# Attention over two layers: image 0 starts from centred values, and the last checks move ahead of the last residual

## The chip, the cores and the metric

The kernel runs on one core of a Trainium2 chip. A core has TensorE for matrix products, VectorE, ScalarE and GpSimd for work on elements, and a sync engine, SP, that here only issues transfers. The engines run side by side, each through its own list of instructions in order, and wait for one another by semaphores. Products land in PSUM; everything else lies in SBUF. The metric is the time of one execution on the device, in microseconds. Smaller is better.

## The reference

The input `x` holds 16 images of 256 channels by 32 x 32 places. Two layers of the same form follow, each with its own weights:

```python
x = x + attention(group_norm(x), Wq, bq, Wk, bk, Wv, bv, rel_h, rel_w)

def group_norm(v, G=16, eps=1e-5):       # groups lie along the last axis
    g = v.reshape(B, H, W, G, C // G)
    m = mean(g, axis=(1, 2, 4)); s = var(g, axis=(1, 2, 4))
    return (g - m) / sqrt(s + eps)

def attention(x):                         # 4 heads of depth 64, n = 1024 places
    q, k, v = Wq @ x + bq, Wk @ x + bk, Wv @ x + bv
    sim = einsum('bhdi,bhdj->bhij', q, k)
    qpos = einsum('hdi,bhdj->bhij', rel_h + rel_w, q)
    return v @ softmax(sim + qpos).T
```

All is float32. The axis that the norm groups is the image's last one, of 32, so a group takes two columns of the picture in all channels.

## The kernel before

A unit is one image in one layer: 32 units, in an order (`units`, line 141) that begins with images 0 to 3 in layer 0. A unit has two pairs of heads, a pair two halves of 512 queries; so a unit has four blocks, and `block(n)` (line 619) writes down the work of one. All instructions are recorded in the order in which the code calls them (`tc.manual_schedule`), and each engine runs its own in that order. Nothing is rearranged.

In a block, `seed` (line 344) has VectorE write the positional part of 128 rows of scores into PSUM, `scores` (line 373) has TensorE add q times k on top and ScalarE take the exponential, and `add_up` (line 397) sums the exponentials on VectorE. `attend` (line 409) multiplies the exponentials by the values. The next block's or unit's projections are put between these by `prepare` (line 593): `project` (q and k, line 258), `values` (line 286), `positions` (line 314). Each is cut in two stretches. A second stretch waits for a `token`, a small GpSimd memset that waits for the first stretch (`stretches`, line 157). PSUM is used as four buffers of two banks with the tags a, b, c and d, handed round in the order of the list `ring`.

The group norm of a unit is prepared one or two units ahead, in pieces on ScalarE: sums of a group (`norm_sums`), squares around the mean (`norm_squares`), and the scaling itself (`norm_apply`). The sums over partitions are small products with a constant matrix (`norm_mean`, `norm_var`), and the power of −0.5 is taken on GpSimd (line 237).

Units 0 and 1 cannot be prepared so. Lines 840 to 959 are the start. SP issues the loads in the order image 0, Wq and Wk of layer 0, image 1, both layers' Wv, Wq and Wk of layer 1, then the small ones and image 2. VectorE sums image 0's halves (`reduced`), two products give the mean (`first_mean`), ScalarE negates it and takes squares of 10 groups, VectorE centres all values and takes the squares of 6. The variance, the power (line 901) and the scaling of the centred values follow (lines 924 to 930), and only then `q(0)` (line 938), the first projection. The weights come untransposed; `transposed` turns them on TensorE and `taken` has ScalarE copy them to SBUF. Image 1's mean and variance are done in the same way in this start, half of its squares on VectorE, and its values are applied by ScalarE in blocks 0 and 1; image 2's sums are ScalarE's in the same blocks.

The last two blocks have a version of their own, `block_without_pieces` (line 762). In the last one, TensorE sums the last exponentials into `pd`. VectorE takes the reciprocal of them (line 827), ScalarE copies them to `d`, and SP sends two rows of `d` to `den_all`, where all softmax denominators are kept. VectorE then ends the last half of the residual (`finish_half`, line 556), which is stored, and checks that the denominators lie in range (`in_range`, line 565). A product over partitions counts the good ones, and a cast writes `flag` (line 837). All engines load the flag; if a denominator was out of range, `general_path` does everything again in a slower way.

Of the kernel before, what the change touches and what calls it, by code (L numbers as in the profile page):

```python
# [9 lines left out]
F32 = mybir.dt.float32  # L10
# [7 lines left out]
P = 128  # L18
# [34 lines left out]
def fast_path(ctx, tc, sh, x, layers, out, W, den_all, token, good, flag):  # L53
# [67 lines left out]
    def transposed(tag, raw, parts):  # L121
        ps = psum2(tag, raw.name + "_t")
        for a in range(2):
            for cc in range(CC):
                for oc in range(CC):
                    nc.tensor.transpose(
                        ps[:, a, cc * C + oc * P : cc * C + (oc + 1) * P],
                        raw[:, a, oc * C + cc * P : oc * C + (cc + 1) * P],
                        W.ident,
                    )  # L130
        for a, which in enumerate(parts):
            raw_t[which] = ps[:, a, :]

# [60 lines left out]
    def norm_sums(u, gs):  # L194
        if u not in reds:
            reds[u] = small.tile([P, G], F32, tag="red", name=f"red_{u}")
        for g in gs:
            of_group(u, g, AF.Identity, reds[u])
# [27 lines left out]
    def norm_squares(u, gs):  # L226
        for g in gs:
            of_group(u, g, AF.Square, sums[u], bias=negs[u][:, g : g + 1])
# [16 lines left out]
    def norm_apply(u, gs):  # L245
        rstd, shift = rss[u]
        for g in gs:
            nc.scalar.activation(  # L248
                grouped(xns[u], g),
                grouped(xt[units[u][0]], g),  # L250
                AF.Identity,
                bias=shift[:, g : g + 1],
                scale=rstd[:, g : g + 1],
            )
# [142 lines left out]
    def add_up(blk, j):  # L397
        u, pr, half = blk
        if j == 0:
            return  # L400
        if j == 1:
            accs[blk] = apool.tile([P, 2, HALF], F32, tag="acc", name=f"acc_{u}_{pr}_{half}")
            nc.vector.tensor_tensor(accs[blk], probs[blk, 0], probs[blk, 1], ALU.add)  # L403
        else:
            nc.vector.tensor_tensor(accs[blk], accs[blk], probs[blk, j], ALU.add)  # L405
# [150 lines left out]
    def finish_half(u, pr, half, o, rden):  # L556
        b, l = units[u]
        columns = slice(half * HALF, (half + 1) * HALF)
        xs = xt[b][:, pr, columns]
        y = outs[u, pr][:, half, :]  # L560
        nc.vector.tensor_tensor(y, o, rden, ALU.mult)
        nc.vector.scalar_tensor_tensor(xs, y, W.bv[l][:, pr : pr + 1], xs, ALU.add, ALU.add)
        nc.sync.dma_start(flat(out[b, pr * P : (pr + 1) * P])[:, columns], xs)
# [24 lines left out]
    ring = ["b", "c", "a", "d"]  # L588
# [29 lines left out]

    def block(n):
# [27 lines left out]
        for j in range(1, 4):  # L647
            scores(blk, j)
        (first, first_out), (second, second_out) = prepare(u, b)
        first(0)  # L650
        if b == 0 and one:
            norm_apply(u + 1, range(0, 1))
        if b == 1 and two:
            norm_sums(u + 2, range(9, 11))
# [3 lines left out]
        if b == 0 and one:  # L658
            norm_apply(u + 1, range(1, 5))
        if b == 1 and two:  # L660
            norm_sums(u + 2, range(11, 12))
        if b == 2 and two:
            norm_squares(u + 2, range(0, 5))
# [21 lines left out]
        add_up(blk, 2)  # L685
        if half == 0:
            second(1)
            second_out()
# [13 lines left out]
        if b == 0 and one:  # L702
            norm_apply(u + 1, range(5, 9))
        if b == 0 and two:
            norm_sums(u + 2, range(0, 2))
        if b == 1 and two:
            norm_sums(u + 2, range(12, G))
        if b == 1 and one:
            norm_apply(u + 1, range(9, 11))
        if b == 2 and two:  # L710
            norm_squares(u + 2, range(5, 11))
# [8 lines left out]
        if after:  # L720
            scores(after, 0)
        values_of_p.word()
# [10 lines left out]
        if two and half == 1:  # L733
            mean_out()
# [10 lines left out]
        if b == 0 and two:  # L745
            norm_sums(u + 2, range(2, 9))
        if b == 1 and one:
            norm_apply(u + 1, range(11, G))
        if b == 2 and two:
            norm_squares(u + 2, range(11, G))  # L750
# [11 lines left out]
    def block_without_pieces(n, half):  # L762
# [61 lines left out]
        finish_half(u, pr, 0, outs[u, pr][:, 0, :], rdens[u, pr][:, :HALF])  # L824
# [3 lines left out]
        d = ppool.tile([P, 2, HALF], F32, tag="p", name=f"d_{n + 1}")[:, 0, :]  # L828
# [3 lines left out]
        finish_half(u, pr, 1, po[:, :, :QUART], rden)  # L832
# [3 lines left out]
        nc.tensor.matmul(pc, good[:, 3:4], W.ones[:, 0:1], start=True, stop=True)  # L836
        nc.vector.tensor_copy(flag, pc)


    load_x(0)  # L840
    raw0 = load_raw("raw0", [(0, "Wq"), (0, "Wk")])
    load_x(1)
    raw1 = load_raw("raw1", [(0, "Wv"), (1, "Wv")])
# [8 lines left out]
    def spread(t, g0=0, g1=G):  # L852
        return (
            t[:, g0:g1].unsqueeze(1).unsqueeze(3).to_broadcast([P, CC * sh.W, g1 - g0, GT])
        )

    def reduced(u, cc):
        nc.vector.tensor_reduce(
            reds[u][:, cc, :],
            xt[units[u][0]][:, cc, :].rearrange("p (w g t) -> p g w t", g=G, t=GT),  # L860
            AX.XY,
            ALU.add,
        )

    def first_mean(u, pm):
        red = reds.pop(u)
        for cc in range(CC):
            nc.tensor.matmul(pm, W.avg, red[:, cc, :], start=(cc == 0), stop=(cc == CC - 1))
        negs[u] = small.tile([P, G], F32, tag="neg", name=f"neg_{u}")
        nc.scalar.mul(negs[u], pm, -1.0)  # L870
        sums[u] = small.tile([P, G], F32, tag="sum", name=f"sum_{u}")
        xns[u] = gnpool.tile([P, CC, N], F32, tag="gn", name=f"xn_{u}")

    def centred(u, g0, g1):
        nc.vector.tensor_tensor(
            by_group(xns[u], g0, g1),
            by_group(xt[units[u][0]], g0, g1),
            spread(negs[u], g0, g1),
            ALU.add,
        )  # L880

    def rest_of_squares(u, g0):

        sq = ppool.tile([P, 2, HALF], F32, tag="p", name=f"first_sq_{u}")
        sq = sq.rearrange("p a n -> p (a n)")[:, : CC * sh.W * (G - g0) * GT].rearrange(
            "p (w g t) -> p w g t", g=G - g0, t=GT
        )
        nc.vector.tensor_tensor(sq, by_group(xns[u], g0), by_group(xns[u], g0), ALU.mult)
        nc.vector.tensor_reduce(
            sums[u][:, g0:], sq.rearrange("p w g t -> p g w t"), AX.XY, ALU.add  # L890
        )

    def first_var(u, pm):
        nc.tensor.matmul(pm, W.avg, sums.pop(u), start=True, stop=True)
        var = small.tile([P, G], F32, tag="var", name=f"var_{u}")
        nc.vector.tensor_scalar(var, pm, EPS, None, ALU.add)
        return var

    def first_rstd(u, var):
        rstd = small.tile([P, G], F32, tag="rstd", name=f"rstd_{u}")  # L900
        nc.gpsimd.tensor_tensor(rstd, var, W.mhalf[:, :G], ALU.pow)  # L901
        return rstd

    for u in range(2):
        reds[u] = small.tile([P, CC, G], F32, tag="first_red", name=f"first_red_{u}")
    G1, G2 = G // 2 + 2, G // 4
    pm0 = psum2("c", "pm_0")
    for cc in range(CC):
        reduced(0, cc)
    first_mean(0, pm0[:, 0, :G])  # L910
    transposed("a", *raw0)
    norm_squares(0, range(G1))
    centred(0, 0, G)
    rest_of_squares(0, G1)
    rstd0 = first_rstd(0, first_var(0, pm0[:, 1, :G]))
    taken(raw0[1])
    transposed("b", *raw1)
    taken(raw1[1])
    pm1 = psum2("d", "pm_1")
    for cc in range(CC):  # L920
        reduced(1, cc)
    first_mean(1, pm1[:, 0, :G])
    transposed("a", *raw2)
    for g in range(G2):
        nc.scalar.activation(
            grouped(xns[0], g), grouped(xns[0], g), AF.Identity, scale=rstd0[:, g : g + 1]
        )
    nc.vector.tensor_tensor(  # L928
        by_group(xns[0], G2), by_group(xns[0], G2), spread(rstd0, G2), ALU.mult
    )  # L930
    taken(raw2[1])
    norm_squares(1, range(0, G // 2))
    centred(1, G // 2, G)
    rest_of_squares(1, G // 2)
    (q, q_out), (k, k_out) = (
        project(0, 0, which, psum2(tag, f"p{which}_0_0")) for which, tag in (("q", "b"), ("k", "c"))
    )
    q(0)
    k(0)
    q(1)  # L940
    q_out()
    k(1)
    k_out()
    ab, ab_out = positions(0, 0, psum2("a", "pa_0_0"))
    ab(0)
    ab_out()
    var1 = first_var(1, pm1[:, 1, :G])
    for j in range(3):
        seed(blocks[0], j, ring[j])
    v, v_out = values(0, 0, psum2("d", "pv_0_0"))  # L950
    v(0)
    scores(blocks[0], 0)
# [3 lines left out]
    rstd1 = first_rstd(1, var1)  # L956
    shift1 = small.tile([P, G], F32, tag="nshift", name="nshift_1")
    nc.vector.tensor_tensor(shift1, negs.pop(1), rstd1, ALU.mult)
    rss[1] = (rstd1, shift1)
# [282 lines left out]
```

## Time and profile before

| What | us |
|---|---|
| Median of 3 runs (2536.82 to 2538.13) | 2537.84 |
| The profiled execution | 2537.8 |
| Its span, first instruction to last | 2535.9 |
| TensorE products busy in the span | 2512.9 (99%) |
| VectorE busy | 2267.8 (89%) |
| ScalarE busy | 1949.0 (77%) |
| GpSimd busy | 834.1 (33%) |
| First product of q | at 18.09 |
| Last product of values | ends at 2526.06 |
| Flag written | at 2530.28 |

Times in a trace are microseconds from the start of the span. A row of the timeline has the start, the length, the engine, the line, the operation with what it writes and reads, how many were merged, and in brackets how long the engine had been idle before and what ended that. PE is TensorE, PEld its weight loads, DVE is VectorE, ACT is ScalarE, POOL is GpSimd, and SPq the issue of a transfer. An fp32 product leaves two records. The chain of waits goes back from the last instruction, at each step to what released it.

The landing of the first transfers, from the trace (issue, and from issue to landing): image 0's halves 0.75 + 3.7 and 1.2 + 4.5, Wq 1.67 + 4.9, Wk 2.15 + 5.5, image 1's first half 2.66 + 6.3, the first Wv 3.66 + 7.3.

### The profile page before, as it was taken

Reading aid. Unit: us, or ns where it says so; the run is one execution under the profiler, and the core shown is the slowest. Engines: PE = TensorE matmul, PEld = TensorE weight load, DVE = VectorE, ACT = ScalarE, POOL = GpSimd, SP = SyncE. Lnnn points to the kernel's source line nnn. Section 1 sums busy time; section 2 is a strip of 40 time slices with the busy share of each in tenths; the row PEclk is TensorE's granted clock in tenths of the full one; section 3 lists DMA queues with packets and bytes.
Section 4 is the critical chain, followed back from the end, with each engine's and each line's share of the span. In section 5 each row is a group of like instructions: output and inputs, shape, how many; then the busy total and the mean of one; then the engine's idle time right before and its main releaser. Section 6 shows DMA issues by size and latency. Waiting matters only on the chain.

```text
span 2535.9 us, 85952 instructions
## 1 busy us (share of the span) xinstructions
PE 2512.9 (99%) x37462; PEld 1332.5 (53%) x37462; DVE 2267.8 (89%) x2133; ACT 1949.0 (77%) x3876; POOL 834.1 (33%) x1195
## 2 busy tenths in 40 slices
PE   8999999999999999999999999999999999999998
PEld 4555555555555555555555555555555555555554
DVE  6898998989989989899899899998998999989997
ACT  6778777787777887777877778877778777787654
POOL 1333333323333233333233332333323333323320
PEclk9999999999999999999999999999999999999999
DMA  3344443544444445444444444444454444444442
GB/s 90 74 79 75 87 87 67 101 96 93 96 90 104 80 76 101 88 84 95 92 88 94 79 97 81 85 104 90 87 112 81 90 79 84 80 84 77 95 81 69
DMA packets 119841, 221.57 MB, mean 87 GB/s; under 512 B 53913, under 2 KB 55449, under 8 KB 119457
## 3 DMA queue, kind: packets, MB, share of 16 engines
q0 software_dynamic: 53712, 130.10, 31.4%
q1 hardware_dynamic: 65744, 85.90, 12.0%
q8 instruction: 295, 4.83, 0.8%
q14 instruction: 90, 0.73, 0.1%
HBM read 51.78 MB, written 17.30 MB: 27 GB/s over the span
## 4 chain that ended last, share of the span: by engine, by line
PE 97%; DVE 1%; DMA 1%; POOL 1%; issue 1%; SPq 0%; ACT 0%; POOLq 0%; DVEq 0%; ACTq 0%
PE ps L385 34%; PE po L419 34%; PE pk L268 9%; PE pv L298 9%; PE pq L268 9%; PE pa L326 2%; DMA stack<-stack 0%; DMA den_all<-d 0%; PE pm L209 0%; DMA x<-in_x_dram 0%; DVE acc L405 0%; DVE rden L827 0%; POOL rstd L237 0%; POOL rstd L901 0%; POOL stack L460 0%
## 5 line engine op out<-in xcount | busy, mean ns | idle before, releaser
L349 DVE TENSOR_TENSOR ps<-abt 128x1024 f32<-128x1024 f32 x1018 | 1228.8, 1230 | 230.3 <-ACT p L394 144.3
L394 ACT ACTIVATE p<-ps,shift 128x1024 f32<-128x1024 f32 x1024 | 1091.3, 1114 | 335.4 <-PE ps L385 335.4
L385 PE MATMUL ps<-q,k 64*64 64x512 f32 x8192 | 985.9, 590 | 0.0
L419 PE MATMUL po<-p,v 64*64 64x256 f32 x16384 | 930.5, 376 | 0.0
L419 PEld LDWEIGHTS po<-p,v 64*64 64x64 f32 x16384 | 629.1, 133 | 364.3 <-issue 77.2
L405 DVE TENSOR_TENSOR acc<-acc,p 128x1024 f32<-128x1024 f32 x643 | 780.4, 1214 | 8.2 <-ACT p L394 1.4
L385 PEld LDWEIGHTS ps<-q,k 64*64 64x64 f32 x8192 | 306.6, 133 | 397.9 <-issue 274.9
L166 POOL MEMSET token<- 1x1 f32 x320 | 36.2, 113 | 1033.5 <-PE po L419 469.9
L465 POOL DMA_DIRECT2D stack<-stack x310 | 255.0, 823 | 196.0 <-DMA stack<-stack 109.4
L298 PE MATMUL pv<-Wv,xn 64*64 64x256 f32 x4096 | 244.3, 376 | 0.6 <-POOL token L166 0.3
L268 PE MATMUL pq<-xn,Wq 64*64 64x512 f32 x2048 | 243.8, 591 | 0.3 <-DVE xn L928 0.3
L268 PE MATMUL pk<-xn,Wk 64*64 64x512 f32 x2048 | 242.8, 589 | 0.0
L460 POOL DMA_DIRECT2D stack<-acc x248 | 221.6, 1075 | 41.6 <-issue 30.0
L248 ACT ACTIVATE xn<-x,nshift,rstd 128x128 f32<-128x128 f32 x496 | 210.3, 496 | 1.1 <-POOL nshift L239 1.1
L298 PEld LDWEIGHTS pv<-Wv,xn 64*64 64x64 f32 x4096 | 153.5, 133 | 102.7 <-issue 51.6
L436 POOL DMA_DIRECT2D acc<-p x124 | 118.8, 958 | 247.3 <-ACT od L480 162.3
L190 ACT ACTIVATE junk<-x,neg 128x128 f32<-128x128 f32 x498 | 195.2, 400 | 0.0
L480 ACT COPY od<-po 128x512 f32<-128x512 f32 x127 | 74.3, 585 | 114.9 <-PE po L419 114.9
L403 DVE TENSOR_TENSOR acc<-p,p 128x1024 f32<-128x1024 f32 x128 | 155.8, 1217 | 0.0
L441 POOL DMA_DIRECT2D acc<-acc x124 | 106.0, 855 | 148.3 <-DMA acc<-p 139.3
L268 PEld LDWEIGHTS pq<-xn,Wq 64*64 64x64 f32 x2048 | 78.6, 134 | 142.1 <-issue 133.2
L190 ACT ACTIVATE junk<-x 128x128 f32<-128x128 f32 x480 | 145.0, 311 | 0.0
(75 smaller groups left out, 1124.5 us busy)
## 6 DMA issues: line engine op xcount, KB each, us to landing
acc<-p POOLq DMA_DIRECT2D x124, 512.0 KB, 5.7
rden<-rd SPq DMA_DIRECT2D x126, 256.0 KB, 6.0
acc<-acc POOLq DMA_DIRECT2D x124, 256.0 KB, 3.6
x<-in_x_dram SPq DMA_DIRECT2D x32, 512.0 KB, 4.3
stack<-acc SPq DMA_DIRECT2D x248, 64.0 KB, 2.1
stack<-acc POOLq DMA_DIRECT2D x248, 64.0 KB, 3.0
out_dram<-x SPq DMA_DIRECT2D x31, 512.0 KB, 3.8
stack<-stack POOLq DMA_DIRECT2D x62, 128.0 KB, 4.2
```

The costliest lines, as they stand in the source:

```text
L190: nc.scalar.activation(junk, grouped(xt[units[u][0]], g), func, accum_out=into[:, g : g + 1], **bias)
L248: nc.scalar.activation(grouped(xns[u], g), grouped(xt[units[u][0]], g), AF.Identity, bias=shift[:, g : g + 1], scale=rstd[:, g : g + 1],)
L268: yield nc.tensor.matmul(pk[c, nh, :], w[l][rs, cc, c0 : c0 + D], xns[u][rs, cc, nh * HALF : (nh + 1) * HALF], start=(t == 0 and cc == 0), ...
L298: yield nc.tensor.matmul(pv[c, a, i, :], xns[u][rs, cc, j0 : j0 + D], W.wv[l][rs, cc, :], start=(t == 0 and cc == 0 and i == 0), stop=(t = ...
L349: nc.vector.tensor_tensor(ps.rearrange("p h (w y) -> p h w y", y=H), ab[:, :, :H].unsqueeze(2).to_broadcast([P, 2, XH, H]), ab[:, :, H + h ...
L385: nc.tensor.matmul(ps[c, h, :], a[hs, j0 : j0 + D], b[hs, columns], start=bool(tag) and i == 0, stop=i == len(terms) - 1, skip_group_check ...
L394: nc.scalar.activation(p, ps, AF.Exp, bias=W.shift)
L403: nc.vector.tensor_tensor(accs[blk], probs[blk, 0], probs[blk, 1], ALU.add)
L405: nc.vector.tensor_tensor(accs[blk], accs[blk], probs[blk, j], ALU.add)
L419: yield nc.tensor.matmul(po[c, a, :QUART], vts[u][rs, j, c0 : c0 + D], p[rs, h, a * QUART : (a + 1) * QUART], start=(t == 0 and j == 0), s ...
L460: nc.gpsimd.dma_start(at, acc[R:D, h, :], accum_op=ALU.add)
L465: nc.gpsimd.dma_start(stack[:rows_], stack[rows_ : 2 * rows_], accum_op=ALU.add)
```

## The change

At the start:

- SP loads both Wv before image 1.
- `transposed` becomes a generator, `transposes`. Wq's transposes stand between the two products of the first mean, Wk's behind the second.
- `q(0)` and the other three projection stretches of unit 0 read the centred, not the scaled values. The scaling by 1/sqrt(var) is a VectorE product from PSUM to SBUF per 512 columns (`scaled`), and the bias is added in place by ScalarE (`biased`). This is possible because a column of q or k depends on one column of the values alone, and a column lies in one group.
- The centred values themselves are scaled by VectorE in two halves (`first_scaled`), before `values` reads them.
- ScalarE takes squares of 9 groups, not 10, and copies Wq and Wk in between them.
- Image 1's mean is taken by `norm_mean`; all its squares are ScalarE's, 3 groups in the start and 13 in block 0. Its variance is taken in block 0 and its values are applied in block 1 alone.
- Image 2's sums are VectorE's: a reduction in block 0, one in block 1.
- The transposes of layer 1's Wq and Wk come behind the positions of unit 0.
- Tags: `ring` starts as c, a, b, d.

In the blocks, the calls for the norms are gathered in `norms(u, b, i)` with tables. From unit 1 on they are the old ones, but that in a unit's first block two sums come ahead of four applies.

At the end, the check of the denominators and the product that counts them come before the last half's residual. The cast of the flag comes between that residual's two VectorE instructions. `d` takes a buffer of another pool.

```diff
 def norm_apply(u, gs):
-        rstd, shift = rss[u]
         for g in gs:
+            rstd, shift = rss[u]
...
+    APPLY = {0: (0, 1, 5, 9, 9), 1: (9, 9, 9, 11, G)}
+    SUMS = {0: (0, 0, 0, 2, 9), 1: (9, 11, 12, G, G)}
+    SQUARES = {2: (0, 0, 5, 11, G)}
+    FIRST_SQUARES = {0: (3, 5, 9, G, G)}
+    FIRST_APPLY = {1: (0, 1, 4, 8, G)}
+
+    def norms(u, b, i):
+        def groups(table):
+            return range(*table.get(b, (0,) * 5)[i : i + 2])
+        if u == 0:
+            norm_squares(1, groups(FIRST_SQUARES))
+        elif u + 2 < NU:
+            norm_sums(u + 2, groups(SUMS))
+        if u + 1 < NU:
+            norm_apply(u + 1, groups(APPLY if u > 0 else FIRST_APPLY))
+        if u + 2 < NU:
+            norm_squares(u + 2, groups(SQUARES))
...
-        for j in range(1, 4):
+        for j in range(1 if n > 0 else 2, 4):
             scores(blk, j)
         (first, first_out), (second, second_out) = prepare(u, b)
         first(0)
+        norms(u, b, 0)
+        if n == 1:
+            reduced(2, 1)
+            added(2)
         seed(blk, 4, f1)
         scores(blk, 4)
         add_up(blk, 1)
+        norms(u, b, 1)
...
         add_up(blk, 2)
+        if n == 0:
+            reduced(2, 0)
...
         if after:
             scores(after, 0)
+        if n == 0:
+            mean_out = norm_var(1, filled(f1, f"pm_{n}", EPS / 2))
         values_of_p.word()
...
         rden = rdens[u, pr][:, HALF:]
         nc.vector.reciprocal(rden, pd)
-        d = ppool.tile([P, 2, HALF], F32, tag="p", name=f"d_{n + 1}")[:, 0, :]
+        d = apool.tile([P, 2, HALF], F32, tag="acc", name=f"d_{n + 1}")[:, 0, :]
         nc.scalar.copy(d, pd)
         for hs in QUARTERS:
             nc.sync.dma_start(den_all[hs, n, :], d[hs.start : hs.start + 1, :])
-        finish_half(u, pr, 1, po[:, :, :QUART], rden)
         list(in_range(flatden[:, 8 * (n - 1) :], 2))
         nc.vector.tensor_reduce(good[:, 3:4], good[:, 0:3], AX.X, ALU.min)
         pc = psum2(f1, "pc")[0:1, 0, 0:1]
         nc.tensor.matmul(pc, good[:, 3:4], W.ones[:, 0:1], start=True, stop=True)
+        steps = finish_half(u, pr, 1, po[:, :, :QUART], rden)
+        next(steps)
         nc.vector.tensor_copy(flag, pc)
+        list(steps)
...
     load_x(0)
     raw0 = load_raw("raw0", [(0, "Wq"), (0, "Wk")])
+    raw1 = load_raw("raw1", [(0, "Wv"), (1, "Wv")])
     load_x(1)
-    raw1 = load_raw("raw1", [(0, "Wv"), (1, "Wv")])
...
+    def scaled(into, t, rstd):
+        shape = dict(g=G, t=GT)
+        nc.vector.tensor_tensor(
+            into.rearrange("p (w g t) -> p w g t", **shape),
+            t.rearrange("p (w g t) -> p w g t", **shape),
+            spread(rstd, XH),
+            ALU.mult,
         )
...
+    def first_mean(pm, between):
+        part = parts.pop(0)
         for cc in range(CC):
+            nc.tensor.matmul(pm, W.avg, part[:, cc, :], start=(cc == 0), stop=(cc == CC - 1))
+            next(between)
...
+    pm0 = psum2("d", "pm_0")
     for cc in range(CC):
         reduced(0, cc)
+    first_mean(pm0[:, 0, :G], transposes("a", *raw0))
+    transposed("b", *raw1)
+    norm_squares(0, range(4))
     taken(raw0[1])
+    norm_squares(0, range(4, G // 2 + 1))
+    nc.vector.tensor_tensor(
+        by_group(xns[0]), by_group(xt[0]), spread(negs[0], CC * sh.W), ALU.add
+    )
+    rest_of_squares(G // 2 + 1)
+    pq, pk = psum2("c", "pq_0_0"), psum2("a", "pk_0_0")
+    q, k = project(0, 0, "q", pq)[0], project(0, 0, "k", pk)[0]
+    q(0)
+    q.word()
+    nc.tensor.matmul(pm0[:, 1, :G], W.avg, sums.pop(0), start=True, stop=True)
+    var = small.tile([P, G], F32, tag="var", name="var_0")
+    nc.vector.tensor_scalar(var, pm0[:, 1, :G], EPS, None, ALU.add)
+    rstd = small.tile([P, G], F32, tag="rstd", name="rstd_0")
+    nc.gpsimd.tensor_tensor(rstd, var, W.mhalf[:, :G], ALU.pow)
+    taken(raw1[1])
     for cc in range(CC):
         reduced(1, cc)
+    added(1)
+    pm1 = filled("d", "pm_1", 0.0)
     k(0)
     q(1)
     k(1)
+    kqs = {}
+    for which, bias, ps in (("q", W.bq, pq), ("k", W.bk, pk)):
+        t = kqs[which] = kqpool.tile([P, N], F32, tag=which, name=f"{which}_0_0")
+        for nh in range(NH):
+            scaled(t[:, nh * HALF : (nh + 1) * HALF], ps[:, nh, :], rstd)
...
+    biased("q", W.bq, 0)
+    biased("q", W.bq, 1)
+    biased("k", W.bk, 0)
+    qs[0, 0], ks[0, 0] = kqs["q"], kqs["k"]
+    mean_out = norm_mean(1, pm1)
+    ab, ab_out = positions(0, 0, psum2("b", "pa_0_0"))
     ab(0)
     ab_out()
+    biased("k", W.bk, 1)
+    mean_out()
...
+    first_scaled(0)
+    transposed("d", *raw2)
+    taken(raw2[1])
+    seed(blocks[0], 0, ring[0])
+    scores(blocks[0], 0)
+    seed(blocks[0], 1, ring[1])
+    seed(blocks[0], 2, ring[2])
     v, v_out = values(0, 0, psum2("d", "pv_0_0"))
     v(0)
+    norm_squares(1, range(3))
+    first_scaled(1)
+    scores(blocks[0], 1)
     v(1)
     v_out()
     seed(blocks[0], 3, ring[0])
```

## The prediction

> **What bounds the kernel now.** I read the chain of waits first, then the busy time by stretches, and only then the start and the end in order of time. The page's chain:
>
> ```profile
> PE 97%; DVE 1%; DMA 1%; POOL 1%; issue 1%; SPq 0%; ACT 0%; POOLq 0%; DVEq 0%; ACTq 0%
> ```
>
> Busy time by stretches (stretch, its length, then each engine's busy us and count, clock, DMA):
>
> ```profile
> 0.00:20.00 20.00, 9.91 (x46) 7.79 (x50) 13.20 (x15) 11.01 (x40) 3.62 (x7) 1.00 0.71 235
> ...
> 180.00:2400.00 2220.00, 2219.62 (x33308) 1173.80 (x33304) 2006.23 (x1885) 1742.80 (x3505) 763.68 (x1084) 1.00 0.45 88
> ...
> 2520.00:2536.00 16.00, 6.25 (x86) 3.07 (x77) 8.08 (x11) 0.58 (x1) 0.09 (x1) 0.78 0.20 71
> ```
>
> TensorE works 2219.62 of 2220 us in the middle. No edit there can give or take anything unless it stops TensorE. So a change is worth what it does before TensorE first runs without a break and after its last product. The chain at the start (start, us, what):
>
> ```profile
> 1.21 4.55 DMA x<-in_x_dram
> ...
> 7.92 2.30 DVE xn L875
> ...
> 11.24 0.96 DVE sum L889
> ...
> 13.22 2.94 POOL rstd L901
> ...
> 16.19 1.77 DVE xn L928
> ...
> 18.09 2.99 PE pq L268 x16
> 21.09 1.72 PE pk L268 x16
> ...
> 35.03 1.73 PE pv L298 x32
> ```
>
> From 18.09 us TensorE hardly waits again; until then it waits for image 0's normalisation, whose longest links are the power on GpSimd and the scaling after it. I use 35.03 us, where block 0's second value product begins, as a milestone: the work behind it is the same in both kernels. The end, in order of time:
>
> ```profile
> 2525.94 0.58 ACT L829 COPY d<-pd 128x512 f32<-128x512 f32 x1 [7.50 <-DVE rden L827]
> 2526.55 1.12 SPq L831 DMA_DIRECT2D den_all<-d  x2
> ...
> 2527.76 0.54 SPq L563 DMA_DIRECT2D out_dram<-x  x1
> 2528.98 0.17 DVE L568 TENSOR_SCALAR range<-den_all 128x16 f32<-128x16 f32 x1 [1.38 <-DMA den_all<-d]
> ...
> 2530.13 0.15 DVE L837 CAST flag<-pc 1x1 int32<-1x1 f32 x1 [0.37 <-PE pc L836]
> ```
>
> The last residual and its store run while VectorE would wait for `den_all` anyway. Between the flag (2530.28) and the end of the span (2535.94) lie 5.66 us, in which all engines load the flag and branch; TensorE's branch alone took 3.92.
>
> **What the Trainium skill says.** (1) "TensorE: Matmul & The Clock Gate", Part 1: TensorE runs at half rate until a free-running window of about 3.4 us has been busy. The trace agrees: the first stretch of q, 16 records, took 2.81 us (18.09 to the next group's 20.90), the following ones 1.72. (2) "VectorE: DVE Perf Modes", Why PSUM operands drop a tier: fp32 runs at one element a cycle from PSUM. The trace agrees: 128x512 products took 0.684 us from SBUF and 0.691 from PSUM, so scaling q and k in PSUM costs no more than elsewhere. (3) "GPSIMD Engine Reference", table of specifications: GpSimd shares SBUF interfaces with VectorE, and VectorE instructions with two SBUF inputs contend. The trace fits: the power took 2.93 us beside reductions, 3.54 beside seeds, and 4.06 in the median later. In the new start it again stands beside reductions, so I take 2.94.
>
> **The change part by part, the start.** Up to the first half's mean product (5.76) nothing changes.
> *Wq's transposes between the halves.* They are put in front of the second mean product in TensorE's order. Wq was issued at 1.67 and landed 4.9 us later, at 6.57. Eight transposes took 1.95 us, so 0.22 each; with a weight load of 0.21 ahead, four end at 7.72. The second mean product goes from 7.06 to 7.72: −mean starts at 8.36, not 7.70. Loss 0.66. Bounds: 0 if Wq lands at 6.0, 1.2 if at 7.1.
> *Wv ahead of image 1 on SP.* The bytes are the same; Wv lands where image 1's first half did (8.96 before), image 1 by about 11.8. Wv's transposes then follow Wk's without a wait: 0.44 for the mean product, 12 x 0.22, ends at 10.8. Image 1 is wanted only at 14. Cost nothing; if Wv came 1 us late, q would start 0.5 late.
> *q starts on centred values.* Centring takes 2.29: 8.58 to 10.87. Four squares at 0.39 and Wq's copy end at 10.7. q's first stretch starts at 10.95 instead of 18.09: 7.1 us earlier. How long it takes depends on the clock: 1.72 full, about 3.4 half. TensorE is dense from 6.84, so a full busy window ends between 10.0 and 13.5; I take 12.3, thus 2.4 us, to 13.35.
> *The variance.* ScalarE now has nine squares and both copies, ending 13.15, VectorE's seven groups 13.1; both are covered by q. The variance product queues behind q: 13.35, 0.6 with its result, var 0.17, power 14.2 to 17.15. k's and q's stretches cover it: 13.8 + 2 x 1.72 = 17.25. k's second stretch waits for a token that stands behind the power on GpSimd: 17.4 to 19.1.
> *Scale and bias after the product.* Added are four VectorE products (0.6 apart, from L561's row) and four ScalarE biases of 0.57, for two of 1.11. q's halves are ready at 19.35 and hold the positions (from 19.4, after 0.26 for image 1's mean) by nothing; they end at 20.3. k's halves, the abt copy (1.0) and k's last bias lie behind one another on ScalarE: 20.6, 21.6, 22.1. VectorE scales half of xn (2 x 0.6) before the first seed: 22.0 to 23.2. So TensorE, which had no gap here before, has one from 20.3 to 23.25, of which Wq1's and Wk1's moved transposes fill at most 1.8.
> *From there.* Scores 0.86, values 1.72, scores 0.86; the second value stretch waits for xn's other half behind two seeds (23.2 + 2 x 1.14 + 1.25 = 26.7), 1.73; two scores 1.72: 30.15 at the milestone, 4.9 us ahead of 35.03.
> *Image 1's squares and applies, image 2's sums in blocks 0 and 1.* Seven squares (2.73) behind the last exponential hold the new variance product by 0.2, and it takes 0.26. VectorE gets two reductions of 1.21 each. Block 0's stands ahead of seed 6, and VectorE idled 1.81 us before seed 7: covered. Block 1's stands ahead of seed 4, where 1.95 idled; but VectorE enters block 1 later too, since seeds 1 to 3 now stand behind the reduction of the variance, which waits for its product. Together seeds 6 and 7 come about 0.95 later against TensorE, and they had 0.7 and 0.4 of slack: 0.6 lost. About 1.1 in all; between 0.3 and 1.6. The two reordered ScalarE pieces in later units (sums ahead of four applies) have cover from 4.3 us of products and cost nothing.
> Sum of the start: −4.9 + 1.1 = −3.8.
>
> **The end.** The copy `d` still waits for the reciprocal: both read `pd`, and in both built orders its wait is on VectorE alone; its new pool's older transfers are long done. So `den_all` lands as before and the checks still start at 2528.98. Now the product (0.69) stands ahead of the flag's cast, less the 0.37 that the cast waited for `pc`: flag 0.4 later. The store, issued at 2527.76 before, follows at about 2531.6 behind SP's flag load; with 2.2 us to landing it ends at 2533.8, and SP's closing waits by about 2535, when TensorE's branch ends too. Cost 0.5; bounds 0.3 and 1.5.
> Total −3.8 + 0.5 = −3.3. The profiled execution took 2537.8 with its span of 2535.9, so 1.9 lie around it, and it equals the median of 2537.84: 2534.5 us. That is 0.13%; 0.2%, or 5.1 us, is about what a measurement of this kernel can tell from no change, so I call it within.
>
> **Rivals.**
> *More at the start.* If Wq lands early (−0.6), block 1's seeds fit into VectorE's 1.95 us of idle there (−0.6) and the clock is free at 10 (−0.2), then −4.7 to −5.8: about 2532.4. For it: those are the terms that I bound widest. Against it: the late variance takes up most of that idle.
> *Clock stays low through the projections.* Half the records before 12.3 are transposes, and no earlier busy stretch of 2.2 us released it. If it comes at 19, three stretches cost up to 1.7 more each, partly inside the later gap: about 2 more, 2536.6.
> *Slower.* The gap from 20.3 to 23.25 splits the work. If only an unbroken window releases the clock, it comes at 27 or later, and everything from 10.95 to there runs at half rate: 11 us of products double, less the gaps they fill. That gives +3, 2540.8; past a release at about 22 us it decides, and each further half-rate window of 3.4 us costs 1.7. Against it: before, it was released 2.2 us after the projections began, across small gaps.
> *No effect*, that q does not begin earlier, is excluded by the order: its waits are on xn, Wq and nothing of the power.
>
> **Numbers.** Forecast 0.57, more 0.28, low clock 0.09, slower 0.06. The forecast's own range is 2533.2 to 2536.0; with the low clock and about half of the rival with more, 0.8 lie in 2532.0 to 2536.9. Faster 0.28, within 0.2% 0.68 (slower's milder part included), slower 0.04.
>
> **What would show it.** q's first product near 11 us; scores 0 near 23.3; the second value product of block 0 near 30.2; waits for seeds 6 and 7 in block 1 of 0.2 to 0.3; the flag about 5.7 us ahead of the end, the store behind it. Wrong would be: q's records at 0.43 spacing only after 13.5, a wait of TensorE for Wq beyond 0.9 us, a new gap anywhere after 60 us, or a flag earlier against the last product than the 4.1 us of before.

## The result

The changed kernel takes 2531.66 us (median of 15 runs, 2530.88 to 2533.56); the kernel before, on the same chip, 2537.64 us (2536.55 to 2538.55). The ratio is 0.9977 with a 95% interval of 0.997 to 0.9984: 5.98 us faster, 0.24%. The forecast was 2534.5, and the wider of its two ranges began at 2532.0: the time lies 0.34 us below it. The profiled execution took 2531.66 us with a span of 2529.9, so 1.8 us lie around it, about as before.

The page's chain of waits, and the busy time by stretches (stretch, length, then busy us and count of TensorE's products, TensorE's weight loads, VectorE, ScalarE and GpSimd; granted clock, DMA share, GB/s), of the changed kernel:

```profile
PE 96%; DVE 2%; DMA 1%; issue 1%; POOL 0%; SPq 0%; ACT 0%; DVEq 0%; POOLq 0%
```

```profile
0.00:20.00 20.00, 13.26 (x159) 8.07 (x159) 12.73 (x20) 9.11 (x28) 3.77 (x9) 1.00 0.71 238
180.00:2400.00 2220.00, 2219.62 (x33304) 1173.75 (x33300) 2006.28 (x1884) 1744.73 (x3507) 765.14 (x1086) 1.00 0.45 88
```

The middle is what it was, to the hundredth: 2219.62 us of work in 2220. In the first 20 us TensorE's products are busy for 3.35 us more. The chain at the start of the changed kernel, in order of time (start, us, what):

```profile
1.67 4.69 DMA raw<-in_L_conv_Wq_dram
...
7.58 0.26 PE pm L898 x2
7.86 0.19 ACT neg L901
8.08 1.67 ACT junk L194 x8
...
13.13 1.88 PE pk L272 x16
...
16.72 1.71 PE pk L272 x16
19.11 0.68 DVE k L871
19.89 1.20 DVE xn L871 x2
21.09 1.15 DVE ps L353
22.29 1.09 PE ps L389 x8
...
29.40 1.73 PE pv L302 x32
```

The chain leaves out q itself, which the order in time has (start, us, instruction, idle time before it and what ended it):

```profile
10.52 1.95 PE L272 MATMUL pq<-xn,Wq 64*64 64x512 f32 x16 [0.29 <-DVE xn L925]
```

q starts 0.15 us after the centred values are there, and at full rate: the record of the clock has it from 9.84 us on. That moment is called the release of the clock below. The milestone, block 0's second value product, stands at 29.40 instead of 35.03. To see where the two traces part, I took the start of each block's products with p in both (block 0 to 127) and subtracted. A gain made once stays as a constant, so the steps of this curve are where time went or came from:

| products with p of | before | after | difference |
|---|---|---|---|
| block 0 | 45.17 | 39.55 | -5.62 |
| block 1 | 63.31 | 58.40 | -4.91 |
| block 2 | 84.06 | 79.16 | -4.91 |
| block 64 | 1291.05 | 1286.14 | -4.91 |
| block 126 | 2494.71 | 2489.80 | -4.91 |
| block 127 | 2516.84 | 2509.38 | -7.46 |
| end of the span | 2535.94 | 2529.88 | -6.06 |

So: -5.6 up to block 0's products, +0.7 from there to block 1's, nothing for 125 blocks, then **-2.55 between the products of the last two blocks, a stretch that no edit touches**, and +1.4 at the end, 0.83 of it behind the flag. Start and end together, -3.5, are close to the forecast's -3.3. The miss sits in the last blocks. There the chain of the kernel before reads

```profile
2486.66 3.23 DMA stack<-stack
...
2501.88 0.06 DVE r L515
...
2506.77 1.22 DVE acc L405
...
2508.14 1.55 PE po L490 x8
```

and that of the changed kernel

```profile
2481.83 2.16 DMA stack<-stack
...
2496.07 0.06 DVE r L519
...
2500.97 1.22 DVE acc L409
```

Both run from the last fold of the stacked sums, an 8 KB accumulating transfer (L465 before, L469 after), over SP's transfers to `den_all` and VectorE's reciprocals and additions to TensorE's sums of p. The fold took 3.23 us before and 2.16 after; everything behind it came 1 us earlier. TensorE's wait there, before:

```profile
PE po L490 <- DVE range L568: 2.6, 1, 2.6
```

and after:

```profile
PE po L494 <- DVE range L573: 1.9, 1, 1.9
```

In the kernel before, the clock also fell after that wait (two stretches, columns as above):

```profile
2505.40:2508.20 2.80, 0.15 (x6) 0.09 (x4) 2.70 (x5) 1.34 (x2) 0.00 (x0) 1.00 0.98 237
2508.20:2512.00 3.80, 3.80 (x20) 1.32 (x24) 3.77 (x5) 0.58 (x1) 0.00 (x0) 0.55 0.41 87
```

The clock's record has half rate from 2508.57 for 3.41 us: 1.7 us of TensorE's work lost. In the changed kernel it stays full to 2522. Counted from block 126's products, the sums of p start 0.89 earlier (12.54 us after them, for 13.43). With the full clock's 1.7 that makes up the 2.55.

Why was the fold faster? The transfers of the two traces in the 1.3 us around it (queue, then packets, MB, share), before and then after:

```profile
q0 software_dynamic: 32, 0.01, 6.0%
q8 instruction: 1, 0.02, 5.4%
```

```profile
q0 software_dynamic: 32, 0.01, 5.8%
```

In the kernel before, a 16 KB load of instructions lies on the fold; in the changed kernel it does not. The trace has 295 such loads for 75,040 TensorE records, one per 254, so nearly all of them seem to be TensorE's program: 4.83 MB are 64 bytes per record, and the other queue of such loads, q14, has 0.73 MB for the 10,912 records of the other engines, 67 bytes each. That is an argument from counts; no trace names the engine. The change adds 5 products at the start, each recorded as two products and two weight loads (image 1's mean and variance by quarters, `mean_of_rows`); after has 75,059 records. My theory after the result: they moved the load off the fold. The rivals: the last blocks' gain is luck of one execution; or the end edit makes it.

The end of the changed kernel, in order of time:

```profile
2518.92 0.59 ACT L840 COPY d<-pd 128x512 f32<-128x512 f32 x1 [7.93 <-DVE rden L838]
...
2521.96 0.18 DVE L573 TENSOR_SCALAR range<-den_all 128x16 f32<-128x16 f32 x1 [3.08 <-DMA den_all<-d]
...
2523.26 0.14 DVE L849 CAST flag<-pc 1x1 int32<-1x1 f32 x1
...
2524.32 0.34 SPq L568 DMA_DIRECT2D out_dram<-x  x1
```

From the flag (2523.40) to the end of the span are now 6.49 us, for 5.66 before.

### The profile page after: what moved, and what is told of

It is laid out like the page before. It is cut to its first block, busy times and chain, and to the rows that moved or that the text cites. A ratio compares the mean times of both kernels' runs of the same rounds, so it can differ in the third digit from the quotient of the medians.

```text
span 2529.9 us, 85967 instructions
## 1 busy us (share of the span) xinstructions
PE 2508.4 (99%) x37472; PEld 1329.7 (53%) x37472; DVE 2270.2 (90%) x2143; ACT 1946.6 (77%) x3855; POOL 835.9 (33%) x1196
## 3 DMA queue, kind: packets, MB, share of 16 engines
q8 instruction: 295, 4.83, 0.8%
## 4 chain that ended last, share of the span: by engine, by line
PE 96%; DVE 2%; DMA 1%; issue 1%; POOL 0%; SPq 0%; ACT 0%; DVEq 0%; POOLq 0%
PE po L423 34%; PE ps L389 34%; PE pv L302 9%; PE pk L272 9%; PE pq L272 8%; PE pa L330 2%; DVE ps L353 1%; DVE acc L409 0%; DMA den_all<-d 0%; PE pm L213 0%; DMA stack<-stack 0%; DMA raw<-in_L_conv_Wq_dram 0%; ACT junk L194 0%; DVE acc L407 0%; POOL rstd L241 0%
## 5 line engine op out<-in xcount | busy, mean ns | idle before, releaser
L469 POOL DMA_DIRECT2D stack<-stack x310 | 254.8, 822 | 179.5 <-DMA stack<-stack 94.7
```

The source lines that it names most:

```text
L469: nc.gpsimd.dma_start(stack[:rows_], stack[rows_ : 2 * rows_], accum_op=ALU.add)
```

## The experiments

The kernel before had a median of 2537.55, 2537.61, 2537.74 and 2537.87 in the four sessions; differences are against that of the same session, with a 95% interval by resampling the runs. A difference to the changed kernel, which ran in the session of the result, is the difference of two such differences. Line numbers differ by a few between the kernels.

**The end alone** (b_end): the kernel before with the changed end (the diff's part in `finish_half` and `block_without_pieces`).

> The kernel before with the end of the changed kernel alone: d's tile from the other pool, range checks and flag's cast ahead of the last residual addition and its store. My prediction's sum gives +0.5 us (flag 0.4 later, the store hidden by TensorE's branch): 2538.1. The trace of the changed kernel instead has 11.28 us from the last product's end to the span's end for 9.88 before: +1.4, 2539.0, with the closing waits of SP held by the store. A rival, that the end edit also does something in the last two blocks, would show a time below 2537.

Measured 2538.86, +1.31 (0.77 to 1.51). In its trace the flag is 0.07 later against the last block's products, and from the flag to the end 6.56 instead of 5.66 us. The forecast's +0.5 lies outside the interval.

**The start alone** (a_oldend): the changed kernel with the end of before.

> The changed kernel with the end of the kernel before: the start alone. The traces differ by -5.62 us at block 0's value products, by a constant -4.91 from block 1 to block 126, by -7.45 at the last block, and by +1.4 after it. If the last blocks' gain of 2.55 belongs to the start edit (its shift against something periodic), this gives 2537.6 - 7.45 = 2530.2. If that gain was luck of the one profiled execution, 2537.6 - 4.9 = 2532.7. By my prediction's sum for the start, -3.8: 2533.8.

Measured 2531.79, -5.77 (-6.24 to -4.79). Its trace again gains 3.0 between block 126 and 127: the last blocks' gain comes with the start edit, and it is no luck of one execution. Its flag comes 14.01 us after the start of block 127's products, as in the changed kernel, for 13.44 before and 13.51 in b_end. So 0.57 of the +1.4 is no cost of the end edit: VectorE, which leads to the flag, followed TensorE's gain only in part. Net, the last blocks gave about 2.0 us in this pair of traces, and start and end edit together 4.1. The end edit seems free in the measured times here; more on that below.

**Filler in TensorE's last wait** (b_fill, a_fill), the same lines in both kernels:

```diff
+            for _ in range(16):
+                nc.tensor.matmul(
+                    pos[n - 1][:R, 0, QUART:], W.ones[:, :R], qs[u, pr][:, :QUART],
+                    start=True, stop=True, tile_position=(0, 0), skip_group_check=True,
+                )
             sums_of_p(blocks[first:n], pos[n - 1])
```

> The kernel before with 16 products of 256 columns (each about 0.11 us, their result overwritten by the sums that follow) ahead of the last block's sums of p, where TensorE idled 2.65 us and its clock then fell to half for 3.41 us. If the half-rate window is what the idle time triggers, the filler (1.7 us of 2.65) prevents it: -1.7 us, 2535.9, and a clock record without the window at 2508. If only the wait for VectorE counts there, nothing changes: 2537.6. Were the wait usually shorter than 1.7 us, it would get slower by up to 0.5.

> The same 16 products in the changed kernel, whose trace idled 1.95 us there and kept the clock full. If the half-rate window never comes in the changed kernel, no change: 2531.7. If it comes in some executions (the two of 15 at 2533.1 and 2533.6), the upper end of the times comes down to about 2532.3 and the median hardly moves.

Measured 2542.31 (+4.76) and 2536.47 (4.9 above the changed kernel). I had mis-sized the filler: the 16 products became 32 records of 0.21 us each, 6.9 us in place of 1.7. The clock stayed full in both traces, but the filler itself outlasted the wait, so this pair says nothing on what the window costs. About 1.9 us of b_fill's 4.76 also lie outside the traced span (3.7 us around it in its 20 runs, for 1.8 before); why is open.

**The load's place, moved in the kernel before** (b_pad, later b_pad2 and b_pad10 with 2 and 10 in place of 5):

```diff
+    for _ in range(5):
+        nc.tensor.matmul(pm0[:, 1, :G], W.avg, W.avg[:, :G], start=True, stop=True)
     centred(0, 0, G)
```

> The kernel before with 5 extra 16-column products (20 TensorE instructions, as many as the change adds; results overwritten) early, where TensorE idles before image 0's variance. Theory of the instruction load: in the three traces with the old start a 16 KB load of TensorE's instructions begins 7.0 to 7.1 us before block 126's value products and overlaps the last fold's transfer, in the three with the new start it begins 8.2 us before them and does not; the fold is then seen 1.0 us earlier, VectorE runs 1.0 us earlier and TensorE's wait for its last sums is 1.5 to 1.95 instead of 2.5 to 2.65 us. So this shifts the load to -8.2, takes 1.0 off the wait and spares the half-rate window in most executions: 2535.5 to 2536.2. If the place of the load has nothing to do with it: 2537.6.

Measured 2535.52, -2.09 (-2.73 to -1.01). Five useless products at the start, far from the end, make the kernel faster. At block 126 its trace is 0.97 behind that of before, and it still reaches the last block's products 1.68 ahead; the fold takes 2.18 us, and the wait is

```profile
PE po L490 <- DVE range L568: 1.8, 1, 1.8
```

**The load's place, moved back in the changed kernel** (a_few):

```diff
+        if whole:
+            nc.tensor.matmul(
+                pm[:, 0, :], W.avg, red, start=False, stop=True, skip_group_check=True
+            )
+            return
         for c in QUARTERS:
...
-        mean_of_rows(pm, reds.pop(u))
+        mean_of_rows(pm, reds.pop(u), u == 1)
...
-        mean_of_rows(pm, sums.pop(u))
+        mean_of_rows(pm, sums.pop(u), u == 1)
```

> The changed kernel with image 1's mean and variance by one whole 128-row product each instead of four quarters each: 24 fewer TensorE instructions, about as many as the kernel before has. By the same theory the load moves back to about -6.9 us, the wait grows to 2.5 us and the half-rate window returns: +1 to +2.7, less 0.2 for the shorter variance product: 2532.5 to 2534.2. If the place of the load has nothing to do with it: 2531.5.

Measured 2534.11, 2.48 (1.38 to 3.69) slower than the changed kernel, although it has less work to do. In its trace fold and wait read

```profile
2482.33 3.88 DMA stack<-stack
```

```profile
PE po L499 <- DVE range L578: 2.6, 1, 2.6
```

and the half-rate window is back. The rivals fall as the cause of the last blocks' gain: it went and came with a few instructions at the start, under either end. Whether a window of half rate follows is another matter, and in part luck; the last section has it.

**Dose** (b_pad2, b_pad10):

> The kernel before with 2 extra products (8 TensorE instructions) instead of 5: the instruction load moves from -7.0 to about -7.5 us before block 126's value products and ends at -6.4, still after the fold's first packets at -6.7. In all six traces where load and fold overlapped, SP went on 1.23 us after the load's end. So here it goes on at about -5.2, 0.5 earlier than before and 0.5 later than with 5 products: 2536.3 to 2537.1. If the number of extra products does not matter in order (any change of the program's place does it): near 2535.5 or 2537.6.

> The same with 10 extra products (40 instructions): the load at about -9.5 us, clear of the fold: as with 5 products, 2535.3 to 2536 (0.3 more at most for the products themselves). If the gain of 5 products came from their work at the start (a clock released earlier) rather than from the load's place, 10 give more: below 2535.

Measured 2537.99 (+0.12, -0.47 to 0.78) and 2538.2 (+0.33, -0.05 to 1.4). Both miss their forecasts; the traces show where the load was in each. Times in us from the start of block 126's products:

| kernel | load of instructions | last fold's data | SP goes on | last wait |
|---|---|---|---|---|
| before | -7.04 to -5.91 | -6.66 to -5.90 | -4.68 | 2.65 |
| b_pad2 | -7.12 to -5.72 | -6.68 to -5.70 | -4.49 | 2.6 |
| a_few | -6.20 to -5.28 | -6.68 to -5.26 | -4.04 | 2.6 |
| b_pad | -8.32 to -7.40 | -6.61 to -6.15 | -5.68 | 1.8 |
| after | -8.25 to -7.33 | -6.60 to -6.14 | -5.68 | 1.95 |
| b_pad10 | -9.04 to -7.92 | -5.16 to -4.70 | -4.24 | 2.5 |

With 2 products the load did not move at all (it does not follow the count evenly), and so nothing changed. With 10 it moved onto the fold before this one: that fold's data was through at -7.91 instead of -8.75, GpSimd issued the last one at -6.55 instead of -8.05, and the chain was as late as ever. In all eight traces with load and last fold overlapping, the fold's last packet ended within 0.02 us of the load, and SP went on 1.23 or 1.24 us after it; without overlap, 0.46 to 0.49 us after the data. In six of the eight, 30 of the fold's 32 packets were through by about -6.2, as without overlap, and only the last two, of 12 bytes together, ended with the load (before: -6.21, then -5.90). That overlap is what counts is shown; why SP then goes on 0.8 us later than after a fold without overlap is not.

**VectorE's other work out of the way** (b_late, a_late): reciprocals, product and addition by DMA from block 126 to behind the last block's first additions.

```diff
-            reciprocals(*summed)
-            normalise(*before)
-            add_by_dma(*before)
...
+        if last:
+            reciprocals(*blocks[n - 2][:2])
+            normalise(*blocks[n - 5][:2])
+            add_by_dma(*blocks[n - 5][:2])
+            nc.gpsimd.drain()
```

> The kernel before with VectorE's reciprocals, the product after them and the addition by DMA moved behind the last block's first three additions of p, so that TensorE no longer waits for them before its sums: the wait of 2.65 us and the half-rate window after it (1.7) go: 2533.2 to 2534.0, if VectorE has room for the moved 1.4 us later in the block. If only the wait goes and the window stays: 2535. With VectorE late at the end: up to 1.4 given back.

> The changed kernel with the same move. Its wait of 1.5 to 1.95 goes, and the window in the executions that have it: 2529.5 to 2530.2. The difference between this and the same move in the kernel before is then the start and the end alone, without the last blocks: -4.1 + 1.3 = -2.8 if the start's mean over the phases of the clock (-4.1 by three traces of each start) and the end's cost measured alone add up; -3.3 by my prediction; -6 if the last blocks have no part in the result.

Measured 2537.96 (+0.35, -0.2 to 0.98) and 2533.09 (1.5 slower than the changed kernel, 0.5 to 2.3). The wait did go, and the last products of the kernel before came 4.1 us earlier against block 126. But VectorE had the moved work still ahead of it, and the flag came 3.35 later behind them: all given back. TensorE's and VectorE's ends lie close together in the last block, and one gains only while the other follows. In b_pad and the changed kernel VectorE itself is 1 us earlier, so most of the 2.55 stays.

**Wq's transposes behind both mean products** (a_mean2):

```diff
-            next(between)
+        list(between)
```

> The changed kernel with both halves' mean products ahead of Wq's transposes, as before, and nothing else. My prediction put the transposes' place at a loss of 0.66 us (bounds 0 to 1.2): the same products then start -mean, centring, q and scores 0 about 0.6 us earlier, 2531.0. If the start hangs on something else by then (Wq's copy on ScalarE, the squares) or the clock is released later because the transposes no longer fill TensorE's first window: 2531.7 to 2532.2.

Measured 2532.06, +0.3 (-0.7 to 1.3) against the changed kernel: no gain. In its trace -mean starts 0.25 earlier (7.61), but q starts at 10.99, 0.47 later: 16 transposes from 7.41 on now stand ahead of q on TensorE. In the changed kernel four of them fill the time in which TensorE waits for the second half's sum anyway. The clock was released at 11.38 here, but five traces of the new start in which it was released later have q at 10.41 to 10.83, so the clock is not the reason.

**The flag's cast behind the addition** (b_flaglast): the checks ahead of the residual as in b_end, but with `finish_half` whole and ahead of the cast, and `d` in its old pool.

> The kernel before with the range checks ahead of the last residual addition as in the changed kernel, but the flag's cast behind the addition. The end edit alone cost 1.31 us. In its trace the flag was only 0.08 later against the last product, and the closing took 6.56 instead of 5.66 us: the store was issued behind SP's load of the flag and its landing held SP's last four waits. If that is the cause, here the flag is 0.75 later and the store is issued ahead of its load again, so the closing is 5.7 to 6.0: 2538.4 to 2538.7. If the flag's cast is what counts: 2539.2 or more.

Measured 2538.69, +0.95 (0.35 to 1.57). In the traces the flag is 0.9 later than before and the closing takes 5.92. The table shows the closing in all kernels but a_dfirst_old, which follows below (us from the flag's end):

| order | last store issued at | end of the span |
|---|---|---|
| old (before, b_pad, b_pad2, b_pad10, b_fill, b_late, a_few_old, a_oldend) | -2.5 | 5.66, 5.72, 5.83, 5.66, 5.80, 5.96, 5.83, 6.06 |
| cast last (b_flaglast) | 0.0 | 5.92 |
| new (b_end, b_pad_end, after, a_mean2, a_few, a_fill, a_late, a_dfirst) | 0.92 | 6.56, 6.35, 6.49, 6.52, 6.97, 6.61, 6.63, 6.81 |

In the first row the span ends 1.1 to 1.2 us after TensorE's branch. In the last it ends 1.8 to 2.0 after it: the store's landing decides, since SP's closing waits stand behind it. Issued ahead of the flag or with it, the store takes 2.0 to 2.2 us to landing; issued 0.92 after it, 3.5 to 4.1. Why it is slower there was not tested.

**The end crossed with the load's place** (b_pad_end: b_pad with the changed end; a_few_old: a_few with the end of before):

> The kernel before with 5 extra products and the changed kernel's end. The end edit cost 1.31 us on the kernel before and -0.13 in the changed one. If its cost is its own (store behind the flag's load), 2535.5 + 1.3 = 2536.8. If it vanishes where the last blocks run faster (VectorE is then the late engine and the flag 0.5 later in either order), 2535.5 to 2535.8.

> The changed kernel with 24 fewer TensorE instructions (load at -6.2, the half-rate window back) and the kernel before's end: the start edit alone with no gain in the last blocks. If the end edit costs 1.3 whenever the load is late: 2534.1 - 1.3 = 2532.8. If it is free with the new start, whatever the load does: 2534.1.

Measured 2537.07, 1.29 (-0.05 to 2.13) above b_pad; and 2533.89, where the changed end costs 0.48 (-0.46 to 1.65). With the old start the end edit costs 1.3, wherever the load is. With the new start it costs -0.2 (-1.5 to 0.8) and 0.5 us in the two pairs. The intervals overlap, and the traces of both pairs have the closing longer by 0.4 and 1.1; whether the cost is really smaller there stays open.

**d ahead of the reciprocal** (a_dfirst; a_dfirst_old with the end of before). VectorE's reciprocal of 128x512 takes 3.35 us, against 0.69 for a product of that shape, and `d`, which starts the last chain to the flag, was copied behind it:

```diff
-        nc.vector.reciprocal(rden, pd)
         d = apool.tile([P, 2, HALF], F32, tag="acc", name=f"d_{n + 1}")[:, 0, :]
         nc.scalar.copy(d, pd)
...
+        nc.vector.reciprocal(rden, d)
         list(in_range(flatden[:, 8 * (n - 1) :], 2))
```

> The changed kernel with d copied on ScalarE before VectorE's reciprocal, which then reads d instead of the products' PSUM tile. The reciprocal takes 3.35 us in these traces and the copy waited for it, and with it den_all's transfers, the range checks and the flag. The flag then waits for the reciprocal and the checks on VectorE instead of the transfers' landing: about 2 us earlier, and the store with it: 2529.5 to 2530.2. If the end hangs on the last residual's store by then, only 1 us: 2530.7.

> The same with the kernel before's end: residual addition and store ahead of the range checks. With den_all landed early nothing is waited for between them, so the product and the addition (1.45 us) delay the flag, but the store is issued ahead of the flag's load. By the closing waits' lengths (5.7 to 6.1 behind an early store, 6.5 behind a late one) the flag is 0.75 later than in the version with the checks first and the closing 0.4 to 0.9 shorter: within 0.3 of it. If TensorE's branch alone sets the closing: 0.75 slower.

Measured 2528.80 (5 runs; ratio to before 0.9966, 0.9952 to 0.9979; 2.96 below the changed kernel, 1.82 to 3.87) and 2530.31. The first is the best version here, beating both kernels. The end of a_dfirst:

```profile
2514.85 0.58 ACT L839 COPY d<-pd 128x512 f32<-128x512 f32 x1 [4.05 <-PE pd L581]
...
2515.47 3.35 DVE L842 RECIPROCAL rden<-d 128x512 f32<-128x512 f32 x1
2518.74 0.17 DVE L573 TENSOR_SCALAR range<-den_all 128x16 f32<-128x16 f32 x1
...
2520.03 0.14 DVE L849 CAST flag<-pc 1x1 int32<-1x1 f32 x1
```

`den_all` lands while VectorE works on the reciprocal, and the checks follow without a wait. Here the checks-first order is 1.5 us better than the old one (0.5 to 3.7), more than expected. In the traces the flag comes 10.97 us after the start of block 127's products, for 12.44 with the old order: with nothing to wait for, product and addition only delay it. With five and seven runs, and a window of half rate in the trace of a_dfirst_old alone, the size is less sure than the sign.

## Why the prediction was wrong

**The step that failed** is the first: "a change is worth what it does before TensorE first runs without a break and after its last product". It was supported by stretches from 180 to 2400 us and from 2520 us; for the 120 us between the prediction has no term. There TensorE waits 2.65 us for a chain of small transfers, and what the change did there comes from no edited instruction of that stretch: it comes from where a load of instructions falls, which a few more TensorE instructions at the start moved. Removing that effect from the changed kernel (a_few) leaves -3.5; adding it alone to the kernel before (b_pad) gives -2.1. Against -3.5 the sum of -3.3 was right (the one pair of traces has -4.1, with the earliest release of the clock of nine), but by terms that were each off:

- **Wq's transposes, loss 0.66.** -mean came at 7.86, not 8.36: Wq landed 0.2 earlier (6.36) and the second mean product took 0.26 with its weights loaded ahead. -mean is still 0.16 later than the 7.70 of before, but undoing the new place gained nothing: the transposes have to run before q in any order.
- **q near 11, 2.4 long.** 10.52, and 1.95 long: the clock was free at 9.84, not 12.3 (in the other eight traces of this start at 11.3 to 12.9, so the estimate was fair, and this much was luck). The variance product did queue behind q, but waited for ScalarE's squares too (0.30); the power, 2.93 long as taken, ran from 13.43, 0.8 ahead of the forecast.
- **Gap and milestone.** The gap came as described, through k's scaling, half of xn and the first seed; scores 0 at 22.29 (forecast 23.25), milestone 29.40 (30.15).
- **Blocks 0 and 1, +1.1.** The variance product held block 0 by 0.24 and seeds 6 and 7 of block 1 cost 0.43: +0.71 in the curve.
- **The start's sum** was then -4.9, not -3.8. Of the three terms of the rival "more at the start", Wq's early landing and the early clock came true, block 1's seeds still cost 0.43 of the 0.6. Those terms add up to -1.4 and so to a total of -4.7; the prediction has no term for the rest of that rival's range, to -5.8, so its 2532.4 lies near the result without the reason. Part of the -4.9 is chance. In nine traces with each start, release of the clock fell between 19.1 and 22.5 us (old) and 9.8 and 12.9 (new), and block 126 lay later the later it fell, with small exceptions; on average the new start is 4.7 ahead.
- **The end, +0.5.** By the end edit the flag was 0.07 later (b_end), not 0.4. But the store was taken at 2.2 us to landing and took 3.7, and its landing is not hidden by TensorE's branch: the closing grew by 0.8 to 0.9. Measured alone +1.3, inside the bounds' upper end of 1.5; taking 0.5, near the lower bound of 0.3, was wrong.
- **Low clock, slower.** The clock was free by 12.9 at the latest in every trace of the new start; both rivals fall.

## What to carry to other kernels

A constant difference block by block is the quickest way to find where two traces part; do it before explaining any sum. Where a kernel ends in a chain of small transfers that TensorE waits for, look at what else is on their queues, and at every wait that stands in the trace of before, edited or not: a handful of instructions added anywhere ahead can move an instruction load onto that chain or off it, and was worth more here than half of the edit's own gain. In such a tail copy first what starts the transfers, and let the long VectorE operation run beside them.

## What the hardware showed that was not expected

- A 16 KB load of instructions (0.92 to 1.4 us) delays an 8 KB accumulating transfer that it overlaps: 3.0 to 3.9 us to landing instead of 2.2, seen at SP 1.23 us after the load's end. Two packets of the transfer's 32 can be enough.
- Whether the half-rate window follows depends on how the wait lies against a fixed grid of windows. "TensorE: Matmul & The Clock Gate", Part 1, of the Trainium skill has the window free-running at about 3.4 us; the traces agree: from release to the half-rate window lie 2488.32 us in the kernel before, 729 windows of 3.4133, and the same in four others. If windows of that length are laid from the release through all 18 traces, every full-rate window in which TensorE's products left 1.96 us or more empty is followed by one at half rate (26 of 26), and none with 1.90 us or less (some 13,200). No experiment set out to test this. By the length of the wait alone it is less clear: after waits of 2.5 to 2.65 us half rate came in seven traces of seven (before, b_end, b_flaglast, b_pad2, b_pad10, a_few, a_few_old), after 1.5 to 2.0 us in one of seven. That one, a_dfirst_old, had its 1.96 us in one window; the changed kernel's 1.95 was split by a border into 1.18 and 0.77. So its full clock, 1.7 of the 2.55 us, needed the shorter wait and some luck. Two of its 15 runs, at 2533.14 and 2533.56, lie 1.5 and 1.9 us above its median, about as a window of half rate would put them; no trace of those two was kept.
- Where the clock is released early in the start moves everything behind it by up to 1.8 us between traces of the same start.
